# A mixture-of-experts layer on one core: block outputs added in memory, and the shared expert moved behind the routes

## The chip, the cores and the metric

The kernel runs on one core of one Trainium2 chip. The metric is the device time of the whole kernel in microseconds (us). It is a chain of eight layers (four pairs of a mixing layer and a feed-forward layer); the change touches the last layer only.

## The reference, cut to what matters

The input of the last layer, `x`, is 4096 tokens of 256 numbers. Each token goes to the two of eight experts that score highest, and all tokens go to a shared expert; the sum is normalised and added to `x`.

```
xf = layernorm(x)                                   # 4096 x 256
scores = softmax(xf @ w_router)                     # 8 experts
expert_weights, expert_indices = top_k(scores, 2)
cw[token, expert_indices] += expert_weights
h  = silu(xf @ w1[e]) * (xf @ w3[e])                # hidden 512, each expert e
moe_out = sum_e cw[:, e] * (h @ w2[e])
shared  = silu(xf @ ws1) * (xf @ ws3) @ ws2
out = shared / 3 + moe_out * 2 / 3
x = x + layernorm(out)
```

All numbers are 32-bit floats.

## The kernel before, in words

The 4096 tokens are held as eight batches `b` of 512, each a tile of 128 partitions by 4 rows by 256 (`K.X[b]`). The code is written in program order; the order of the instructions on each engine's queue is set afterwards by a planner that takes what it expects to be ready first. Every engine works through its own queue in that order. The loads and stores are issued from SP's queue, the indirect ones (gather and scatter by a list of row numbers) from POOL's.

`l3_ffn` has four stages.

1. Routes. `route(b)` (L1772) normalises the batch on DVE (L1777), transposes it on PE (`norm_T`, L146, copied out by ACT at L148), multiplies by the router (L1783), and takes softmax and the two best experts on ACT and DVE (L1788 to L1804). In the one-hot tiles `O[0]` and `O[1]` it marks which expert is the first and which the second choice of each token; the two weights times 2/3 stay in `G2[b]`. For the first five batches (`EARLY = 5`) `shared(b, ...)` follows: `experts` with the shared weights (matmuls `gs` at L1740, silu on ACT at L1745, product on DVE at L1746), `down` (matmuls `ys` at L1754), and a copy times 1/3 by ACT into `acc[b]`, a tile that stays on the chip (L1877).
2. Sort. `places()` works out on PE and DVE for every token and choice a row in a list sorted by expert, in which each expert fills whole blocks of 256 rows (`rows`, written at L1857), and the expert of each of the 39 blocks (`ei`, L1870). Then 64 scatters on POOL's queue (L1939) write the normalised rows to `xs` in memory, 128 rows of 1 KB each. Before that `xs`, 39 x 256 rows, is cleared by one store from ACT's queue (L1717). SP loads the 39 expert numbers into registers meanwhile (L1887).
3. Blocks. `block(j, ei)` for 39 blocks: the weights of the block's expert (three loads of 512 KB, L1725) and its 256 rows (`xb`, L1893, which waits for all 64 scatters) are loaded; PE transposes the rows (L1900), `experts` and `down` follow, ACT copies the result out of PSUM (L1907), and POOL's queue stores it to `ys` in memory (L1908).
4. The last three batches' shared expert, with weights loaded anew, the rows transposed anew, and the result laid over the batch's normalised rows (`xnr`); then `combine(b)` for all eight batches: eight gathers from `ys` (L1916), each multiplied by its weight and added by DVE (L1919), and `K.add_norm` (L164 to L174: statistics on DVE, scaling on ACT at L172, addition to `X[b]` on POOL at L174). The batch is stored at L1975.

The PSUM pool of `gs` and `gb` has four buffers, that of `ys` and `yb` two; the tiles `xb` and `yb` have two buffers, the hidden tile of the shared expert one.

An earlier layer, `l1_ffn`, already adds its results to rows in memory: L1250 scatters 128 rows of 1 KB with `compute_op=ALU.add` to `out_d`, once for each of 48 experts, and each of these waits for the one before. Its `late(b)` loads the rows back at L1257.

`K.stats` (L99 to L119) has two ways to the inverse root: three Newton steps on DVE, or, where `K.log_exp` is set, Ln and Exp on ACT (L111, L112) and three small DVE instructions (L113 to L115).

Of the kernel before, what the change touches and what calls it, by code (L numbers as in the profile page):

```python
# [9 lines left out]
F32 = mybir.dt.float32  # L10
# [10 lines left out]
NB = 8  # L21
# [1671 lines left out]
def l3_ffn(K):  # L1693


    nc, tc = K.nc, K.tc
    w = K.W["l3_ffn"]
    wr = w[:, 0:16].rearrange("p (k n) -> p k n", k=2)
# [5 lines left out]
    with ExitStack() as es:  # L1704
        def pool(name, bufs, **kw):
            return es.enter_context(tc.tile_pool(name="f3" + name, bufs=bufs, **kw))
        dr = pool("dr", 1, space=DRAM)
        xs = dr.tile([NBLK * BK, D], F32, name="xs")
        ys = dr.tile([NBLK * BK, D], F32, name="ys")
        cst, wp, sb, s1, s3 = pool("c", 1), pool("w", 2), pool("a", 2), pool("b", 1), pool("d", 3)  # L1710
        pmm = pool("pm", 2, space=PSUM)
        pG = pool("pg", 4, space=PSUM)
        pY = pool("py", 2, space=PSUM)

        zero = cst.tile([P, D], F32, name="zero")
        nc.vector.memset(zero, 0.0)
        cleared = nc.scalar.dma_start(  # L1717
            out=xs.rearrange("(n p) d -> p n d", p=P),
            in_=zero[:, None, :].to_broadcast([P, NBLK * BK // P, D]))

        def load_weights(src, uid, sel):
            ts = []
# [37 lines left out]
            return load_weights([i["l3f_s1"], i["l3f_s3"], i["l3f_s2"]], uid, lambda s: s)  # L1760


        XN, O, G2, acc = [], [], [], []
        for j in range(2):
            O.append(cst.tile([P, E, TT], F32, name=f"O{j}"))
        xTs = {}

        def feature_major(b):
            return K.norm_T(b, s1, pmm, "mm", xn=XN[b])

        def route(b):
            xn = cst.tile([P, NT, D], F32, name=f"xnr{b}")  # L1772
            XN.append(xn)
            x = K.X[b]
            mv, r = K.stats([x[:, n, :] for n in range(NT)], "ln")
            for n in range(NT):
                nc.vector.tensor_scalar(  # L1777
                    xn[:, n, :], x[:, n, :], mv[:, n, 0:1], r[:, n:n + 1], ALU.subtract, ALU.mult)
            t = feature_major(b)
            pl = pmm.tile([P, NT, E], F32, tag="mm", name=f"pl{b}")  # L1780
            for n in range(NT):
                for k in range(2):
                    nc.tensor.matmul(  # L1783
                        pl[:, n, :], lhsT=t[:, k, n * P:(n + 1) * P], rhs=wr[:, k, :],
                        start=(k == 0), stop=(k == 1))
            g = sb.tile([P, NT, E], F32, tag="g", name=f"g{b}")
            m = sb.tile([P, NT], F32, tag="m", name=f"m{b}")
            nc.vector.tensor_reduce(m, pl, AX.X, ALU.max)  # L1788
            nc.vector.tensor_tensor(g, pl, m[:, :, None].to_broadcast([P, NT, E]), ALU.subtract)
            nc.scalar.activation(g, g, AF.Exp)  # L1790
            nc.vector.tensor_reduce(m, g, AX.X, ALU.add)
            nc.vector.reciprocal(m, m)
            nc.vector.tensor_tensor(g, g, m[:, :, None].to_broadcast([P, NT, E]), ALU.mult)
            v8 = cst.tile([P, NT, 8], F32, name=f"v8{b}")
            i8 = sb.tile([P, NT, 8], U32, tag="i8", name=f"i8{b}")
            for n in range(NT):
                nc.vector.max(v8[:, n, :], g[:, n, :])
                nc.vector.max_index(i8[:, n, :], v8[:, n, :], g[:, n, :])
            f8 = sb.tile([P, NT, 8], F32, tag="f8", name=f"f8{b}")
            nc.vector.tensor_copy(f8, i8)  # L1800
            nc.vector.tensor_scalar(v8, v8, 2.0 / 3.0, None, ALU.mult)
            G2.append(v8)
            for j in range(2):
                nc.vector.tensor_tensor(  # L1804
                    O[j][:, :, b * NT:(b + 1) * NT].rearrange("p e n -> p n e"),
                    iota[:, None, :].to_broadcast([P, NT, E]),
                    f8[:, :, j:j + 1].to_broadcast([P, NT, E]), ALU.is_equal)
            return t

        def places():  # L1810
# [40 lines left out]
            for j in range(2):  # L1851
# [4 lines left out]
                r = cst.tile([P, TT], U32, name=f"row{j}")  # L1856
                nc.vector.tensor_copy(r, f)  # L1857
                rows.append(r)
            jt = cst.tile([1, NBLK], I32, name="jt")
            nc.gpsimd.iota(jt, [[1, NBLK]], base=0, channel_multiplier=0)  # L1860
            jf = cst.tile([1, NBLK], F32, name="jf")
            nc.vector.tensor_copy(jf, jt)
            ge = cst.tile([1, NBLK, E - 1], F32, name="ge")
            nc.vector.tensor_tensor(
                ge, jf[:, :, None].to_broadcast([1, NBLK, E - 1]),
                end[0:1, None, 0:E - 1].to_broadcast([1, NBLK, E - 1]), ALU.is_ge)
            ef = cst.tile([1, NBLK], F32, name="ef")
            nc.vector.tensor_reduce(ef, ge, AX.X, ALU.add)
            ei = cst.tile([1, NBLK], I32, name="ei")
            nc.vector.tensor_copy(ei, ef)  # L1870
            return rows, ei

        def shared(b, t, ws, a):
            hT = experts(t, L, ws, f"s{b}")
            for half in range(2):
                ps = down(hT, (2 * half, 2 * half + 1), ws[2], f"s{b}_{half}")
                nc.scalar.activation(  # L1877
                    a[:, 2 * half:2 * half + 2, :], ps, AF.Copy, scale=1.0 / 3.0)

        def after(ins, earlier):  # L1880
            tc.add_manual_dep(
# [1 line left out]
                mybir.DependencyInfo(mybir.DependencyClass.Sync, mybir.DependencyReason.DATA),  # L1883
                reason="rows written by it")

        def block(j, ei):
            e = nc.values_load(  # L1887
                ei[0:1, j:j + 1], engines=[mybir.EngineType.SP], min_val=0, max_val=E - 1)
            ws = load_weights(
                [i["l3f_w1"], i["l3f_w3"], i["l3f_w2"]], f"b{j}",  # L1890
                lambda s: s[bass.ds(e, 1)].rearrange("o d n -> (o d) n"))
            xb = sb.tile([P, 2, D], F32, tag="xb", name=f"xb{j}")
            ld = nc.sync.dma_start(  # L1893
                out=xb, in_=xs[j * BK:(j + 1) * BK].rearrange("(n p) d -> p n d", p=P))
            for sc in sorted_:
                after(ld, sc)
            ps = pmm.tile([P, 2, BK], F32, tag="mm", name=f"pxb{j}")
            for k in range(2):
                for n in range(2):
                    nc.tensor.transpose(  # L1900
                        ps[:, k, n * P:(n + 1) * P], xb[:, n, k * P:(k + 1) * P], K.ident)
            xT = sb.tile([P, 2, BK], F32, tag="xbT", name=f"xbT{j}")
            nc.vector.tensor_copy(xT, ps)
            hT = experts(xT, BK, ws, f"b{j}")
            ps = down(hT, (0, 1), ws[2], f"b{j}")
            y = sb.tile([P, 2, D], F32, tag="yb", name=f"yb{j}")
            nc.scalar.copy(y, ps)  # L1907
            nc.gpsimd.dma_start(  # L1908
                out=ys[j * BK:(j + 1) * BK].rearrange("(n p) d -> p n d", p=P), in_=y)

        def combine(b, a, rows):
            for n in range(NT):
                for j in range(2):
                    y = s3.tile([P, D], F32, tag=f"yg{j}", name=f"yg{b}_{n}_{j}")
                    col = b * NT + n
                    nc.gpsimd.indirect_dma_start(  # L1916
                        out=y, out_offset=None, in_=ys[:, :],
                        in_offset=bass.IndirectOffsetOnAxis(ap=rows[j][:, col:col + 1], axis=0))
                    nc.vector.scalar_tensor_tensor(  # L1919
                        a[:, n, :], y, G2[b][:, n, j:j + 1], a[:, n, :], ALU.mult, ALU.add)  # L1920
            K.add_norm(b, [a[:, n, :] for n in range(NT)], s1)

        EARLY = 5
        ws = shared_weights("sh0")
        for b in range(NB):
            t = route(b)
            if b < EARLY:
                acc.append(cst.tile([P, NT, D], F32, name=f"acc{b}"))  # L1930
                shared(b, t, ws, acc[b])
        rows, ei = places()

        sorted_ = []
        for b in range(NB):
            for n in range(NT):
                col = b * NT + n
                for j in range(2):
                    sc = nc.gpsimd.indirect_dma_start(  # L1939
                        out=xs[:, :],  # L1940
                        out_offset=bass.IndirectOffsetOnAxis(ap=rows[j][:, col:col + 1], axis=0),
                        in_=XN[b][:, n, :], in_offset=None)
                    after(sc, cleared)
                    if sorted_:
                        tc.declare_no_dep(sc.ins, group="f3xs", reason="distinct rows")
                    tc.add_to_no_dep_group("f3xs", sc.ins)
                    sorted_.append(sc)
        for j in range(NBLK):
            block(j, ei)
        ws = shared_weights("sh1")  # L1950
        for b in range(EARLY, NB):
            acc.append(XN[b])
            shared(b, feature_major(b), ws, acc[b])
        for b in range(NB):
            combine(b, acc[b], rows)


LAYERS = (("l0_attn", load_l0_attn, l0_attn), ("l0_ffn", load_l0_ffn, l0_ffn),
# [97 lines left out]
```

## Time and profile before

| what | value |
|---|---|
| time, median of 3 runs | 5448.51 us (5447.48 to 5449.12) |
| the profiled execution's own time | 5451.61 us |
| its span, first to last instruction | 5449.9 us |
| granted TensorE clock, mean over the span | 0.915 |
| PE busy over the span | 4489.4 us, 82% |
| DVE / ACT / POOL busy | 3018.0 / 1886.3 / 1875.6 us |
| last layer: first instruction | about 4624 us |
| 64 scatters of the sort (L1939) | 4785.6 to 4866.4 us |
| first block's first matmul record (L1900) | 4873.9 us |
| last block's last matmul record (L1754) | 5319.5 us |
| end of the span | 5449.9 us |

The last layer is 825.9 us of the span, from 4624.0 to the end. A line such as "L1939 POOL DMA_INDIRECT xs<-xnr,row" gives the line of the code, the engine, the operation and the tiles written and read; a stretch in square brackets is the idle time ahead of the instruction and what ended it. A 32-bit matmul of the program shows as two PE records. The time for which POOL is busy with a DMA is that of issuing it; the data lands later.

### The profile page before, as it was taken

The page shows a single profiled execution, that of the slowest core. Times are in us where ns is not written, and L with a number is a line of the kernel's source. Part 1 is how long each engine was busy: PE and PEld are TensorE (multiplying, and loading weights), DVE is VectorE, ACT ScalarE, POOL GpSimd, SP SyncE. Part 2 cuts the span into 40 slices and gives each one's busy share as a digit, 9 for nine tenths or more (in the row PEclk, how much of TensorE's full clock was granted, in tenths as well). Part 3 has the DMA queues.
Part 4 walks back from the last instruction along what each step waited for, and adds up shares of the span by engine and source line. Part 5 has one row for each costly group of instructions (what it writes and reads, how often), then busy time and mean ns, then how long its engine had stood idle before and what let it go on. Part 6 is the DMA issues. An engine that isn't in the chain of part 4 may idle for free.

```text
span 5449.9 us, 55804 instructions
## 1 busy us (share of the span) xinstructions
PE 4489.4 (82%) x18546; PEld 2726.0 (50%) x18546; DVE 3018.0 (55%) x8220; ACT 1886.3 (35%) x3752; POOL 1875.6 (34%) x1218
## 2 busy tenths in 40 slices
PE   8655888999975978888888899788888887929996
PEld 3334765655554964444444455333333333528883
DVE  6999555467684125554555533377777777211115
ACT  5401324343331323333333224455555553201112
POOL 0001213443433341111111000388888887040005
PEclk9777889999997988999999999899999998969997
DMA  4386501000014960000000000011111111136653
GB/s 117 87 202 147 145 26 41 5 9 5 9 38 131 249 179 8 5 5 4 5 5 1 1 19 0 25 48 47 45 45 44 44 44 64 58 124 185 186 180 95
DMA packets 405477, 364.67 MB, mean 67 GB/s; under 512 B 209762, under 2 KB 338996, under 8 KB 404628
## 3 DMA queue, kind: packets, MB, share of 16 engines
q1 hardware_dynamic: 364740, 294.03, 19.6%
q0 software_dynamic: 18768, 40.04, 2.6%
q10 hardware_dynamic: 21680, 27.02, 1.5%
q8 instruction: 147, 2.41, 0.2%
q14 instruction: 142, 1.16, 0.1%
HBM read 279.35 MB, written 81.43 MB: 66 GB/s over the span
## 4 chain that ended last, share of the span: by engine, by line
PE 30%; DVE 15%; issue 12%; POOL 6%; ACT 5%; DMA 1%; POOLq 0%; DVEq 0%; another core or an unknown queue 0%; ACTq 0%; SPq 0%
DVE h L1667 6%; PE T L1402 4%; PE S L1379 3%; PE h L1234 3%; PE g L1495 3%; PE y L1638 3%; DVE junk L1384 2%; DVE dB L1613 2%; PE py L185 2%; POOL h L1670 2%; PE pc L1560 2%; PE y L1245 2%; PE o L1411 1%; ACT PT L1405 1%; PE gs L1740 1%
## 5 line engine op out<-in xcount | busy, mean ns | idle before, releaser
L1670 POOL TENSOR_TENSOR h<-h,C 128x1024 f32<-128x1024 f32 x256 | 595.7, 2354 | 176.0 <-DVE h L1667 140.1
L1638 PE MATMUL y<-h,C 128*128 128x512 f32 x1024 | 533.3, 662 | 106.4 <-POOL h L1670 106.4
L1667 DVE TENSOR_TENSOR_SCAN h<-dA,dB 128x512 f32<-128x512 f32 x512 | 589.0, 1203 | 29.3 <-ACT dA L1664 11.5
L1664 ACT ACTIVATE dA<-dl,A 128x512 f32<-128x512 f32 x512 | 352.6, 691 | 411.0 <-DVE h L1667 400.9
L1638 PEld LDWEIGHTS y<-h,C 128*128 128x128 f32 x1024 | 202.1, 208 | 414.6 <-issue 224.2
L929 POOL TENSOR_SCALAR p<-p,rs 128x128 f32<-128x128 f32 (+3 forms) x256 | 275.7, 1086 | 384.6 <-DVE rs L928 222.1
L1379 PE MATMUL S<-KT,qz 128*128 128x512 f32 (+3 forms) x1024 | 350.1, 479 | 40.9 <-ACT qz L1367 21.3
L174 POOL TENSOR_TENSOR X<-X,yn 128x1024 f32<-128x1024 f32 x64 | 150.7, 2355 | 587.9 <-ACT yn L172 526.8
L1405 ACT ACTIVATE PT<-T 128x256 f32<-128x256 f32 (+3 forms) x512 | 211.4, 437 | 387.0 <-PE T L1402 379.1
L1402 PE MATMUL T<-qz,KT 128*128 128x512 f32 (+3 forms) x1024 | 310.5, 446 | 2.9 <-DVE mx L1384 0.3
L1407 POOL TENSOR_SCALAR_AFFINE_SELECT PT<-PT 128x512 f32<-128x512 f32 x128 | 81.2, 635 | 631.5 <-ACT PT L1405 628.0
L1618 POOL TENSOR_TENSOR dB<-du,B 128x2048 f32<-128x2048 f32 x64 | 289.6, 4526 | 0.1
L1379 PEld LDWEIGHTS S<-KT,qz 128*128 128x128 f32 x1024 | 184.6, 198 | 209.3 <-DVE mx L1384 55.9
L1384 DVE CUSTOM_DVE_ANT_0 junk<-S,mask 128x256 f32<-128x256 f32 (+3 forms) x512 | 250.3, 489 | 61.5 <-PE S L1379 16.2
L1740 PE MATMUL gb<-xbT,w_b 128*128 128x256 f32 x1248 | 277.8, 381 | 7.5 <-issue 7.5
L1740 PEld LDWEIGHTS gb<-xbT,w_b 128*128 128x128 f32 x1248 | 235.9, 190 | 43.1 <-ACT yb L1907 11.4
L1613 DVE TENSOR_TENSOR dB<-du,pb 128x2048 f32<-128x2048 f32 x64 | 145.4, 2273 | 167.7 <-PE pb L1610 118.1
L1402 PEld LDWEIGHTS T<-qz,KT 128*128 128x128 f32 x1024 | 169.9, 191 | 132.8 <-issue 85.1
L1746 DVE TENSOR_TENSOR hTb<-sb,gb 128x512 f32<-128x512 f32 x78 | 53.6, 687 | 298.2 <-PE gb L1740 298.2
L927 ACT ACTIVATE p<-p,nm 128x128 f32<-128x128 f32 (+3 forms) x256 | 143.8, 563 | 197.0 <-DVE nm L923 192.3
L1239 ACT ACTIVATE hT<-h,w_l_ffn 128x128 f32<-128x128 f32 x384 | 109.5, 367 | 221.0 <-PE h L1234 221.0
L1234 PE MATMUL h<-xgT,w 128*128 128x128 f32 x1536 | 185.2, 279 | 0.0
(472 smaller groups left out, 9073.7 us busy)
## 6 DMA issues: line engine op xcount, KB each, us to landing
w_b<-l3f_w SPq DMA_DIRECT2D x117, 512.0 KB
w<-l1f_w SPq DMA_DIRECT2D x48, 1024.0 KB
C<-xdd SPq DMA_DIRECT2D x128, 256.0 KB
B<-xdd SPq DMA_DIRECT2D x64, 256.0 KB
w<-l1f_w SPq DMA_DIRECT2D x48, 256.0 KB
toep<-l0fd SPq DMA_DIRECT2D x32, 320.0 KB
xs<-zero ACTq DMA_DIRECT2D x1, 9984.0 KB
xb<-xs SPq DMA_DIRECT2D x39, 256.0 KB
```

The lines of the kernel that those rows point to most:

```text
L929: nc.gpsimd.tensor_scalar(p[:, 0:n], p[:, 0:n], rs, None, ALU.mult)
L1234: nc.tensor.matmul(ph[:, j, :], lhsT=w1[:, s, c, m * P:(m + 1) * P], rhs=xgT[:, c, :], start=(c == 0), stop=(c == 1))
L1379: nc.tensor.matmul(ps[:, 0:n], lhsT=QZ[:, j, qt * P:n], rhs=KT[:, g, 0:n], start=True, stop=True)
L1384: nc.vector.tensor_tensor_reduce(out=junk[:, 0:n], in0=tiles[j][:, 0:n], in1=mask[:, L - n:L], scale=1.0, scalar=-3.0e38, op0=ALU.add, op1 ...
L1402: nc.tensor.matmul(ps[:, 0:n], lhsT=KT[:, g, kt * P:(kt + 1) * P], rhs=QZ[:, j, kt * P:L], start=True, stop=True)
L1405: nc.scalar.activation(PT[:, j, :], ps[:, 0:n], AF.Exp)
L1618: nc.gpsimd.tensor_tensor(dB, du, B[:, None, :].to_broadcast([P, 4, L]), ALU.mult)
L1638: nc.tensor.matmul(py[2 * j + c], lhsT=K.ident, rhs=h[:, c, :], start=False, stop=(n == NS - 1))
L1664: nc.scalar.activation(dA, dl[:, c, :], AF.Exp, scale=A[:, c, n:n + 1])
L1667: nc.vector.tensor_tensor_scan(hs[-1][:, c % 2, :], dA, dB[:, c, :], 0.0, ALU.mult, ALU.add)
L1670: nc.gpsimd.tensor_tensor(h, h, C[:, None, :].to_broadcast([P, 2, L]), ALU.mult)
L1740: nc.tensor.matmul(ps[:, q, :], lhsT=ww[:, k, (c + q) * P:(c + q + 1) * P], rhs=xT[:, k, :], start=(k == 0), stop=(k == 1))
```

## The change

The last layer is put together in another way.

- The rows that are scattered carry four more numbers each: the token's number, the difference of its two weights, the second weight, and the number of its first expert (`R_ID`, `R_DW`, `R_W1`, `R_E0`). So the rows of `xs`, of `xb` and of the normalised batch are 260 numbers long, 1040 bytes. The cleared rows carry the numbers of padding rows behind the last token.
- There is no `ys` and no `combine`. `acc` is now a list in memory with a row for each token. `shared(b)` stores a third of the shared expert's result there. `block(j)` works out each row's weight (the first choice's if the block's expert is the row's first expert, otherwise the second's), ACT multiplies by it while it copies out of PSUM, in two halves, and two scatters with `compute_op=ALU.add` add the halves to the tokens' rows of `acc`.
- All eight routes come first, then `places()`, the scatters, all eight shared experts, the blocks. The transposed batches of 0 to 4 stay in a pool of five, those of 5 to 7 in a free part of the weights' memory; nothing is transposed twice and the shared weights are loaded once.
- At the end the eight batches of `acc` are loaded and go through `add_norm` with `K.log_exp` set.
- The tiles `xb`, `yb` and the new `wt` and `it` have three buffers.

The diff, cut to its core:

```diff
-        xs = dr.tile([NBLK * BK, D], F32, name="xs")
-        ys = dr.tile([NBLK * BK, D], F32, name="ys")
+        R_ID, R_DW, R_W1, R_E0, R_END = D, D + 1, D + 2, D + 3, D + 4
+        xs = dr.tile([NBLK * BK, R_END], F32, name="xs")
+        acc = dr.tile([NB * L + P, D], F32, name="acc")
+        sx = pool("x", 5)
...
+        nc.sync.dma_start(out=acc[NB * L:NB * L + P, :], in_=zero[:, 0:D])
+        zi = cst.tile([P, 1], I32, name="zi")
+        nc.gpsimd.iota(zi, [[1, 1]], base=NB * L, channel_multiplier=1)
+        nc.vector.tensor_copy(zero[:, R_ID:R_ID + 1], zi)
...
-            t = feature_major(b)
+            dst = spare[:, b - 5] if b >= 5 else None
+            t = K.norm_T(b, sx, pmm, "mm", xn=xn, dst=dst)
...
-            G2.append(v8)
+            nc.gpsimd.tensor_copy(xn[:, :, R_ID], ti[:, b * NT:(b + 1) * NT])
+            nc.vector.tensor_tensor(xn[:, :, R_DW], v8[:, :, 0], v8[:, :, 1], ALU.subtract)
+            nc.gpsimd.tensor_copy(xn[:, :, R_W1], v8[:, :, 1])
+            nc.gpsimd.tensor_copy(xn[:, :, R_E0], f8[:, :, 0])
...
-        def shared(b, t, ws, a):
+        def shared(b, t, ws):
             hT = experts(t, L, ws, f"s{b}")
+            a = sb.tile([P, NT, D], F32, tag="acc", name=f"acc{b}")
             for half in range(2):
                 ps = down(hT, (2 * half, 2 * half + 1), ws[2], f"s{b}_{half}")
                 nc.scalar.activation(
                     a[:, 2 * half:2 * half + 2, :], ps, AF.Copy, scale=1.0 / 3.0)
+            nc.sync.dma_start(
+                out=acc[b * L:(b + 1) * L].rearrange("(n p) d -> p n d", p=P), in_=a)
...
+            xb = s3.tile([P, 2, R_END], F32, tag="xb", name=f"xb{j}")
             ld = nc.sync.dma_start(
                 out=xb, in_=xs[j * BK:(j + 1) * BK].rearrange("(n p) d -> p n d", p=P))
             for sc in sorted_:
                 after(ld, sc)
+            wt = s3.tile([P, 2], F32, tag="wt", name=f"wt{j}")
+            nc.vector.scalar_tensor_tensor(
+                wt, xb[:, :, R_E0], ef[:, j:j + 1], xb[:, :, R_DW], ALU.is_equal, ALU.mult)
+            nc.vector.tensor_tensor(wt, wt, xb[:, :, R_W1], ALU.add)
+            it = s3.tile([P, 2], U32, tag="it", name=f"it{j}")
+            nc.vector.tensor_copy(it, xb[:, :, R_ID])
...
-            nc.scalar.copy(y, ps)
-            nc.gpsimd.dma_start(
-                out=ys[j * BK:(j + 1) * BK].rearrange("(n p) d -> p n d", p=P), in_=y)
+            y = s3.tile([P, 2, D], F32, tag="yb", name=f"yb{j}")
+            for n in range(2):
+                nc.scalar.activation(y[:, n, :], ps[:, n, :], AF.Copy, scale=wt[:, n:n + 1])
+                nc.gpsimd.indirect_dma_start(
+                    out=acc[:, :], out_offset=bass.IndirectOffsetOnAxis(ap=it[:, n:n + 1], axis=0),
+                    in_=y[:, n, :], in_offset=None, compute_op=ALU.add)
...
-        EARLY = 5
-        ws = shared_weights("sh0")
-        for b in range(NB):
-            t = route(b)
-            if b < EARLY:
-                acc.append(cst.tile([P, NT, D], F32, name=f"acc{b}"))
-                shared(b, t, ws, acc[b])
-        rows, ei = places()
+        ws = shared_weights("sh")
+        spare = K.wslot("spare_attn")[:, 0:3072].rearrange("p (b k n) -> p b k n", b=3, k=2)
+        ts = [route(b) for b in range(NB)]
+        rows, ef, ei = places()
...
+        for b in range(NB):
+            shared(b, ts[b], ws)
         for j in range(NBLK):
-            block(j, ei)
-        ws = shared_weights("sh1")
-        for b in range(EARLY, NB):
-            acc.append(XN[b])
-            shared(b, feature_major(b), ws, acc[b])
+            block(j)
+        K.log_exp_tables()
+        K.log_exp = True
         for b in range(NB):
-            combine(b, acc[b], rows)
+            y = sx.tile([P, NT, D], F32, tag="xT", name=f"yl{b}")
+            nc.sync.dma_start(
+                out=y, in_=acc[b * L:(b + 1) * L].rearrange("(n p) d -> p n d", p=P))
+            K.add_norm(b, [y[:, n, :] for n in range(NT)], sb)
+        K.log_exp = False
```

More of the change, by code (lines that the diff above doesn't have):

```diff
@@ L1713, in l3_ffn @@
         pY = pool("py", 2, space=PSUM)
-        zero = cst.tile([P, D], F32, name="zero")
+        zero = cst.tile([P, R_END], F32, name="zero")
         nc.vector.memset(zero, 0.0)
+        nc.sync.dma_start(out=acc[NB * L:NB * L + P, :], in_=zero[:, 0:D])
+        zi = cst.tile([P, 1], I32, name="zi")
+        nc.gpsimd.iota(zi, [[1, 1]], base=NB * L, channel_multiplier=1)
+        nc.vector.tensor_copy(zero[:, R_ID:R_ID + 1], zi)
         cleared = nc.scalar.dma_start(
             out=xs.rearrange("(n p) d -> p n d", p=P),
-            in_=zero[:, None, :].to_broadcast([P, NBLK * BK // P, D]))
+            in_=zero[:, None, :].to_broadcast([P, NBLK * BK // P, R_END]))
+        ti = cst.tile([P, TT], I32, name="ti")
+        nc.gpsimd.iota(ti, [[P, TT]], base=0, channel_multiplier=1)
         def load_weights(src, uid, sel):
@@ L1760, in shared_weights @@
             return load_weights([i["l3f_s1"], i["l3f_s3"], i["l3f_s2"]], uid, lambda s: s)
-        XN, O, G2, acc = [], [], [], []
+        XN, O = [], []
         for j in range(2):
             O.append(cst.tile([P, E, TT], F32, name=f"O{j}"))
-        xTs = {}
-        def feature_major(b):
-            return K.norm_T(b, s1, pmm, "mm", xn=XN[b])
         def route(b):
-            xn = cst.tile([P, NT, D], F32, name=f"xnr{b}")
+            xn = cst.tile([P, NT, R_END], F32, name=f"xnr{b}")
             XN.append(xn)
@@ L1777, in route @@
                 nc.vector.tensor_scalar(
-                    xn[:, n, :], x[:, n, :], mv[:, n, 0:1], r[:, n:n + 1], ALU.subtract, ALU.mult)
-            t = feature_major(b)
+                    xn[:, n, 0:D], x[:, n, :], mv[:, n, 0:1], r[:, n:n + 1], ALU.subtract, ALU.mult)
+            dst = spare[:, b - 5] if b >= 5 else None
+            t = K.norm_T(b, sx, pmm, "mm", xn=xn, dst=dst)
             pl = pmm.tile([P, NT, E], F32, tag="mm", name=f"pl{b}")
@@ L1793, in route @@
             nc.vector.tensor_tensor(g, g, m[:, :, None].to_broadcast([P, NT, E]), ALU.mult)
-            v8 = cst.tile([P, NT, 8], F32, name=f"v8{b}")
+            v8 = sb.tile([P, NT, 8], F32, tag="v8", name=f"v8{b}")
             i8 = sb.tile([P, NT, 8], U32, tag="i8", name=f"i8{b}")
@@ L1858, in places @@
                 rows.append(r)
-            jt = cst.tile([1, NBLK], I32, name="jt")
+            jt = cst.tile([P, NBLK], I32, name="jt")
             nc.gpsimd.iota(jt, [[1, NBLK]], base=0, channel_multiplier=0)
-            jf = cst.tile([1, NBLK], F32, name="jf")
-            nc.vector.tensor_copy(jf, jt)
-            ge = cst.tile([1, NBLK, E - 1], F32, name="ge")
+            jf = cst.tile([P, NBLK], F32, name="jf")
+            nc.gpsimd.tensor_copy(jf, jt)
+            ge = cst.tile([P, NBLK, E - 1], F32, name="ge")
             nc.vector.tensor_tensor(
-                ge, jf[:, :, None].to_broadcast([1, NBLK, E - 1]),
-                end[0:1, None, 0:E - 1].to_broadcast([1, NBLK, E - 1]), ALU.is_ge)
-            ef = cst.tile([1, NBLK], F32, name="ef")
+                ge, jf[:, :, None].to_broadcast([P, NBLK, E - 1]),
+                end[:, None, 0:E - 1].to_broadcast([P, NBLK, E - 1]), ALU.is_ge)
+            ef = cst.tile([P, NBLK], F32, name="ef")
             nc.vector.tensor_reduce(ef, ge, AX.X, ALU.add)
             ei = cst.tile([1, NBLK], I32, name="ei")
-            nc.vector.tensor_copy(ei, ef)
-            return rows, ei
-        def shared(b, t, ws, a):
+            nc.vector.tensor_copy(ei, ef[0:1, :])
+            return rows, ef, ei
+        def shared(b, t, ws):
             hT = experts(t, L, ws, f"s{b}")
+            a = sb.tile([P, NT, D], F32, tag="acc", name=f"acc{b}")
             for half in range(2):
@@ L1884, in after, with block @@
                 reason="rows written by it")
-        def block(j, ei):
+        def block(j):
             e = nc.values_load(
@@ L1891, in block @@
                 lambda s: s[bass.ds(e, 1)].rearrange("o d n -> (o d) n"))
-            xb = sb.tile([P, 2, D], F32, tag="xb", name=f"xb{j}")
+            xb = s3.tile([P, 2, R_END], F32, tag="xb", name=f"xb{j}")
             ld = nc.sync.dma_start(
@@ L1905, in block @@
             ps = down(hT, (0, 1), ws[2], f"b{j}")
-            y = sb.tile([P, 2, D], F32, tag="yb", name=f"yb{j}")
-            nc.scalar.copy(y, ps)
-            nc.gpsimd.dma_start(
-                out=ys[j * BK:(j + 1) * BK].rearrange("(n p) d -> p n d", p=P), in_=y)
[L1911 to L1921, printed above, removed]
-        EARLY = 5
-        ws = shared_weights("sh0")
-        for b in range(NB):
-            t = route(b)
-            if b < EARLY:
-                acc.append(cst.tile([P, NT, D], F32, name=f"acc{b}"))
-                shared(b, t, ws, acc[b])
-        rows, ei = places()
+            y = s3.tile([P, 2, D], F32, tag="yb", name=f"yb{j}")
[8 more added lines that the diff above has]
+        rows, ef, ei = places()
         sorted_ = []
```

## The prediction, put on record before the changed kernel ran

> **What bounds the kernel now.** I read the stage windows of the last layer first, then the timeline of its seams, then the one place earlier in the kernel where the added operation already runs. The columns of the first view are PE, weight loads, DVE, ACT and POOL busy time, the granted clock, DMA share and GB/s.
>
> ```profile
> 4624.00:4785.60 161.60, 140.56 (x516) 91.05 (x516) 58.54 (x339) 41.88 (x65) 0.11 (x1) 0.88 0.19 64
> 4785.60:4873.90 88.30, 0.01 (x1) 0.04 (x1) 0.00 (x0) 0.00 (x0) 61.55 (x64) 0.50 0.39 137
> 4873.90:5319.50 445.60, 437.77 (x2034) 370.90 (x2035) 78.86 (x117) 69.41 (x117) 27.22 (x38) 1.00 0.59 179
> 5319.50:5449.90 130.40, 82.16 (x213) 45.33 (x210) 70.48 (x252) 29.27 (x56) 81.39 (x73) 0.78 0.33 99
> ```
>
> Four stages, each with its own limit: routes with five shared experts (PE), the sort (POOL alone, PE idle), 39 expert blocks (PE, 98%), and three shared experts with the combine, where no engine is full. Together 825.9 us.
>
> ```profile
> 4785.62 1.06 POOL L1939 DMA_INDIRECT xs<-xnr,row  x1 [161.50 <-DVE row L1857]
> ...
> 4865.41 0.96 POOL L1939 DMA_INDIRECT xs<-xnr,row  x1 [0.30 <-issue]
> 4872.37 3.85 SPq L1893 DMA_DIRECT2D xb<-xs  x4
> 4873.89 1.94 PE L1900 MATMUL pxb<-C,xb 128*128 128x128 f32 x8 [93.97 <-DMA xb<-xs]
> ```
>
> The sort is 64 scatters at 1.265 us; PE waits 94 us for its end. SP's 39 register loads (L1887) run beside it, 4785.6 to 4865.4.
>
> ```profile
> 1801.24 1.57 POOL L1250 DMA_INDIRECT out_d<-yw,iT  x1 [0.76 <-DVE yw L1249]
> 1805.81 0.99 POOL L1220 DMA_INDIRECT xg<-xn_d,iT  x1 [2.99 <-PE pxg L1225]
> 1808.17 1.56 POOL L1250 DMA_INDIRECT out_d<-yw,iT  x1 [1.37 <-DMA out_d<-yw,iT]
> ```
>
> L1250 is an accumulating scatter of 128 rows x 1 KB, exactly what the change adds. The third line was held by the first one's data: 6.93 us from start to start, at a DMA share above 0.9.
>
> ```profile
> 5362.11 2.36 POOL L174 TENSOR_TENSOR X<-X,yn 128x1024 f32<-128x1024 f32 x1
> 5362.59 2.18 DVE L1919 SCALAR_TENSOR_TENSOR acc<-yg,v,acc 128x256 f32<-128x256 f32 x1 [1.68 <-DMA yg<-ys,row]
> ...
> 5441.48 2.34 POOL L174 TENSOR_TENSOR X<-X,yn 128x1024 f32<-128x1024 f32 x1 [8.03 <-ACT yn L172]
> 5443.85 0.37 SPq L1975 DMA_DIRECT2D out<-X  x1
> ```
>
> A DVE instruction that usually takes 0.48 us takes 2.18 beside POOL's add; and 6.1 us pass from the last store's issue to the span's end.
>
> **What the Trainium skill says.** "PSUM — Partial Sum Buffer", section Engine vs sequencer instructions: the queues of ScalarE, VectorE and GpSimd are strictly first in, first out. The trace agrees (POOL's 1808.17 line held everything after it). "DMA: Bandwidth & Descriptors", section Rules for kernel authors: an accumulating DMA reads its target and writes it later, so the next one on the same bytes must wait for its semaphore; the 1808.17 line shows that wait. Same page, section Anatomy of one DMA: about 2 us fixed cost, mostly the write receipt; L1250's case (1.56 us of POOL, then 3 to 5 us) is dearer. "SBUF — State Buffer", section Who interferes with whom: a DVE instruction with two SBUF inputs contends with a GpSimd instruction that reads SBUF; the 2.18 us agree.
>
> **The change, part by part** (stage sums against this execution's span of 5449.9; its own time is 5451.6, so 1.7 lie around the span; the median of the runs, 5448.5, is 3.1 below its own time).
>
> *Routes.* Four shared experts leave this stage. One costs PE 32 gs matmul records of 0.43 (13.7 us) and 32 ys records of 0.215 (6.9): 20.6; the period of a route with its shared expert is 23.9 (4656.3, 4680.1, 4704.0), a route being some 3.2. So 4 x 20.7 = 82.8 off, 78.8 left. What is late next: in the built order shared expert 0 stays woven into the routes, so ACT alternates between silu and exp for four rounds (table load 1.28 each way, L1745 and L1790) and each route waits on ACT, PE, DVE in turn. 0 to 12 us for that; I take 4. Stage: 83. The clearing of xs took 31 us (4625.3 to 4656.3, trace's DMA packets); even doubled by 1040-byte rows it ends near 4687, before the first scatter at about 4707. The small POOL copies (24 of 128x4) and the two iotas hide under the routes; uncovered, some 0.2 us each, 5 us.
>
> *Sort.* The same 64 scatters and 39 register loads: 88.3. Rows are 1040 bytes instead of 1024. The trace has no such scatter; bounds are 0.96 us (same descriptors) and 1.56 (L1250's price): 0 to +38 us. A gain is excluded, as the number of rows is the same. I take 0. SP's queue now also holds the stores of acc0 and acc1 among the loads; both are ready before, so nothing waits.
>
> *Shared experts under the sort.* The words of the change promise that 147 us of PE work fill the hole. The built order says otherwise: on DVE, the three small weight instructions of blocks 0 to 2 (after's L1914 to L1918), which wait for xb, stand ahead of shared expert 3:
>
> ```
> L1757 TensorTensor hTs2<-ss2_3,gs2_3_1 128x512
> L1914 TensorScalarPtr wt0<-xb0,ef 128x2      [waits for the load of xb0]
> ...
> L1757 TensorTensor hTs3<-ss3_0,gs3_0_1 128x512
> ```
>
> xb0 waits for all scatters. So DVE stands from about expert 2's end until the sort is over; ACT (silu of 3) and PE (out of PSUM buffers: four, two of which only DVE frees) stop behind it. Under the sort lie experts 1, 2 and five eighths of 3's gs. After it remain 5.1 + 6.9 + 4 x 20.7 = 94.8, and 1.2 to restart: 96 us exposed. Nobody else is hurt: POOL is in its scatters, and acc2's store, queued behind xb0 on SP, has two buffers of slack.
>
> *Blocks.* PE work unchanged: 445.6. Per block ACT gets two scaled copies instead of one (some 0.2 us more), DVE three tiny ones (3 x 0.16): both under 20% busy, hidden; uncovered, 39 x 0.7 = 27 us. POOL loses a 0.72 us write and gets two accumulating scatters, each waiting for the one before. Two of them must fit into 445.6 / 39 = 11.4 us, so 5.71 each. From L1250: the 48 starts are 6.3 us apart, mostly unhindered, so usually under 6.3; by the packets the data lands 4.35 us after the start on average (3.35 to 6.2), and the two held ones restarted 1.1 us after landing: 5.4 at a DMA share above 0.9. Here the share is 0.59, some 0.7 with the adds. Bounds 4.4 (quickest landing) and 6.93: 0 to +95 us; a gain is excluded, since PE is full. I take 5.0, hidden. The first weights of block 1 wait for expert 7's last use of theirs; they have 19 us (expert 7's ys, block 0) for a load of about 8.
>
> *Tail.* Gone: three shared experts, 64 gathers, 64 DVE adds: 130.4. New: ACT 0.8; two last adds 2 x 5 = 10; load of yl0 3.8 (an equal load, L1257, took that to its reader); norm with ACT's Ln/Exp: bn 1.7 + 0.5, ACT 0.5, DVE 0.7, ACT 2.1, gaps 0.2: 5.7; POOL's eight adds 2.36 and then seven at a spacing between 2.36 (POOL full) and 5.5 (DVE and ACT shut out during each add); I take 3.3, since the built order lets DVE run two batches ahead: 23.1; store 6.1. Sum 52 (45 to 67).
>
> Sum: 83 + 88.3 + 96 + 445.6 + 52 = 764.9 against 825.9: 61 off. Span 5388.9, own time 5390.6, and at the median's place 3.1 lower: 5387.5 us.
>
> **The rivals.**
> *The adds become the bound (slower side).* Place: POOL's queue in the block stage, 78 serial adds. Point: above 5.71 us each it costs, at (445.6 + 61) / 78 = 6.5 the gain is gone. At the seen 6.93 for all: 78 x 6.93 = 540.5, +95: 5482. For: weight loads come in bursts, and writes of ys in this stage landed up to 6.3 after issue. Against: the mean of 5.4 was reached at a higher DMA share, and three yb buffers even out single late ones. A milder form, 6.0 each, gives +22: 5410.
> *Wider rows cost POOL 1.56 each:* 64 x 0.6 = 38 more sort, only idle PE beneath: 5426.
> *The weight instructions don't hold DVE* (the change does what it says): 147.5 of shared work from the first scatter, 88.3 covered, 59 left instead of 96: 5350. Against: the built order.
>
> **How the numbers follow.** Forecast 0.66 (own range 5367 to 5408: routes -4/+8, tail -7/+15, combined), wide rows 0.12, adds mildly late 0.08, adds beyond 6.5 us 0.07, full cover 0.07. The range 5350 to 5428 leaves out the slow rival, half of the full cover and the tails. About 0.2% (11 us) is what a measurement of this kernel can tell from no change: faster 0.91, same 0.02 (adds near 6.5), slower 0.07.
>
> **What would show it.** Routes: first xs scatter near 4707. Sort: still 1.27 us per scatter. DVE: an idle of some 45 us before wt0, released by xb0's load; shared experts 3 to 7 after it, first block near 4891. Blocks: 22.7 us per pair, POOL idle between adds released by ACT yb; if by the adds themselves, the first rival holds. Tail: some 52 us from PE's last matmul. The prediction is wrong if the scatter price or the adds' spacing leaves its bounds, or if DVE isn't held.

## The result and the profile after

The changed kernel takes 5615.92 us (median of 4 runs, 5615.01 to 5630.74), the kernel before 5448.82 (4 runs): a ratio of 1.0312, 95% interval 1.0295 to 1.033. It is 167 us slower, where 61 us less had been forecast. The profiled execution is the longest of the four, 5630.74 us with a span of 5628.9, which is 179.0 more than the span of before; the table below adds up to these 179, not to 167.

First the stage windows of the changed kernel, cut at the forecast's seams: routes, sort (up to DVE's first weight instruction), shared experts still to do, blocks (first transpose to PE's last matmul), tail. Columns as before: PE, weight loads, DVE, ACT, POOL, granted clock, DMA share, GB/s.

```profile
4629.60:4702.50 72.90, 57.87 (x277) 41.53 (x278) 48.32 (x333) 26.56 (x41) 4.54 (x28) 0.80 0.49 152
4702.50:4787.50 85.00, 42.78 (x132) 24.71 (x130) 4.71 (x7) 7.76 (x13) 61.51 (x64) 0.78 0.38 131
4787.50:4887.50 100.00, 96.61 (x300) 57.87 (x301) 14.82 (x29) 15.52 (x26) 0.00 (x0) 0.96 0.13 40
4887.50:5579.20 691.70, 515.50 (x2029) 425.19 (x2027) 94.52 (x225) 79.01 (x155) 118.33 (x76) 0.85 0.45 114
5579.20:5628.90 49.70, 0.02 (x1) 0.00 (x0) 21.47 (x96) 21.02 (x51) 21.68 (x10) 0.54 0.56 174
```

| term | before | forecast | after | after less before |
|---|---|---|---|---|
| start of the layer | 4624.0 | same | 4629.6 | +5.6 |
| routes | 161.6 | 83 | 72.9 | -88.7 |
| sort | 88.3 | 88.3 | 85.0 | -3.3 |
| shared experts left over | | 96 | 100.0 | +100.0 |
| blocks | 445.6 | 445.6 | 691.7 | +246.1 |
| tail | 130.4 | 52 | 49.7 | -80.7 |
| sum | | | | +179.0 |

Four terms came within some 10 us, and they alone would have made the kernel faster. The whole surprise is in one row: the same 2030-odd matmul records that filled 445.6 us at a clock of 1.00 now take 691.7, with PE busy for 515.5 of them and a mean granted clock of 0.85. The block stage is no longer PE's.

The timeline of the changed kernel over one block, from the middle of the stage, shows the cycle (weight loads left out):

```profile
5212.40 1.55 POOL L1931 DMA_INDIRECT acc<-yb,it  x1 [10.98 <-ACT yb L1930]
...
5218.32 1.56 POOL L1931 DMA_INDIRECT acc<-yb,it  x1 [4.36 <-DMA acc<-yb,it]
...
5219.87 1.03 PE L1765 MATMUL yb<-w_b,hTb 128*128 128x256 f32 x4
5224.28 0.17 DVE L1918 CAST it<-xb 128x2 uint32<-128x2 f32 x1 [6.91 <-DMA acc<-yb,it]
5224.38 0.69 DVE L1757 TENSOR_TENSOR hTb<-sb,gb 128x512 f32<-128x512 f32 x1
5225.12 4.41 PE L1765 MATMUL yb<-w_b,hTb 128*128 128x256 f32 x12 [4.23 <-DVE hTb L1757]
5229.37 7.07 PE L1751 MATMUL gb<-xbT,w_b 128*128 128x256 f32 x32
5229.57 0.84 ACT L1930 ACTIVATE yb<-yb,wt 128x256 f32<-128x256 f32 x2 [10.64 <-PE yb L1765]
5230.32 1.55 POOL L1931 DMA_INDIRECT acc<-yb,it  x1 [10.44 <-ACT yb L1930]
```

Read it from POOL's first line to its last. The block's first add starts at 5212.40; the second waits until the first one's data has landed and starts 5.92 us later; 5.96 us after that a tiny DVE instruction, the copy of row numbers into `it`, starts, and what it waited for was the second add. Directly behind it on DVE stands the second half of the product `hTb`; PE waited 4.23 us for that; then the rest of `yb`, ACT's copy, and the next block's first add at 5230.32. The cycle is closed: 5.92 + 5.96 + 0.84 (to PE's restart) + 4.45 (yb to ACT) + 0.75 = 17.92 us, and over the stage the period is 17.88, against the 11.4 that PE's work takes (445.6 / 39).

The built order of DVE's queue says why (order, tile, waits):

```
L1757 hTb4 (first half)                 [waits PE, ACT]
L1918 it6<-xb6                          [waits both adds of block 3]
L1757 hTb4 (second half)                [waits PE, ACT]
```

`it` has three buffers. The scheduler makes it as soon as `xb` is there, two blocks ahead; so `it6` takes over the buffer of `it3`, and must wait until the adds of block 3 have read it, only one block back. The three buffers are used up by running ahead, and the wait stands in front of work that is due now.

The groups of `yb` matmuls, of the kernel before (L1754) and of the changed one (L1765), and the acc tile's list of those who waited for it (us, times), with the adds' time to landing, give the sum:

```profile
L1754 PE MATMUL yb<-w_b,hTb 128*128 128x256 f32 x624 | 150.9, 386 | 0.3 <-DVE hTb L1746 0.3
L1765 PE MATMUL yb<-w_b,hTb 128*128 128x256 f32 x624 | 228.4, 532 | 167.9 <-DVE hTb L1757 167.9
```

```profile
  DVE it L1918: 263.8, 36
  POOL acc L1931: 105.5, 27
...
DMA to landing us min/median/max: 3.6/5.4/6.8
```

So 167.9 - 0.3 = 167.6 us are holes and 228.4 - 150.9 = 77.5 are the same matmuls taking longer: 245.1 of the 246.1. The second part is the clock. The windows of the changed kernel around one hole:

```profile
5199.00:5202.00 3.00, 2.95 (x14) 2.26 (x12) 0.00 (x0) 0.60 (x1) 1.56 (x1) 1.00 0.39 128
5202.00:5206.30 4.30, 0.00 (x0) 0.00 (x0) 0.77 (x2) 0.00 (x0) 0.00 (x0) 0.78 0.73 185
5206.40:5208.00 1.60, 1.60 (x4) 1.33 (x5) 0.00 (x0) 0.00 (x0) 0.00 (x0) 0.50 0.00 0
...
5210.00:5212.00 2.00, 2.00 (x10) 1.66 (x9) 0.00 (x0) 0.34 (x1) 0.00 (x0) 0.69 0.00 0
5212.90:5215.00 2.10, 2.10 (x10) 1.87 (x11) 0.77 (x3) 0.11 (x1) 1.06 (x1) 1.00 0.74 252
```

A hole of 4.3 us (second line), then half clock for between 4 and 5 us, then full again. The Trainium skill, "TensorE: Matmul & The Clock Gate", Part 1, says that PE falls to half its clock after an idle window of about 3.4 us and comes back after about as long of work. These lines agree roughly; but 3.4 us is no safe limit for a hole, since in the run with plain writes (below) holes of 2.3 us were followed by half clock too.

At the sort's seam the trace has what the forecast read from the built order. DVE stood 57 us for xb0, and PE 45.6 us behind it; the scatters cost what they did:

```profile
4782.26 0.96 POOL L1946 DMA_INDIRECT xs<-xnr,row  x1 [0.30 <-issue]
...
4787.52 0.22 DVE L1914 SCALAR_TENSOR_TENSOR wt<-xb,ef 128x2 f32<-128x2 f32 x1 [56.94 <-DMA xb<-xs]
...
4790.89 7.35 PE L1751 MATMUL gs<-xT,w_sh 128*128 128x512 f32 x12 [45.61 <-DVE hTs L1757]
```

### The profile page after: what moved, and what is told of

Read it like the earlier page. It is cut to its first block, busy times and chain, and to the rows that moved or that the text cites. A ratio compares the mean times of both kernels' runs of the same rounds, so it can differ in the third digit from the quotient of the medians.

```text
span 5628.9 us, 55853 instructions
## 1 busy us (share of the span) xinstructions
PE 4546.7 (81%) x18522; PEld 2767.8 (49%) x18522; DVE 2994.8 (53%) x8201; ACT 1895.7 (34%) x3800; POOL 1911.0 (34%) x1220
## 5 line engine op out<-in xcount | busy, mean ns | idle before, releaser
L1765 PE MATMUL yb<-w_b,hTb 128*128 128x256 f32 x624 | 228.4, 532 | 167.9 <-DVE hTb L1757 167.9
L1931 POOL DMA_INDIRECT acc<-yb,it x78 | 121.4, 1557 | 681.3 <-ACT yb L1930 405.2
L1765 PEld LDWEIGHTS yb<-w_b,hTb 128*128 128x128 f32 x624 | 167.5, 275 | 218.1 <-DVE hTb L1757 183.5
L1613 DVE TENSOR_TENSOR dB<-du,pb 128x2048 f32<-128x2048 f32 x64 | 145.5, 2274 | 171.3 <-PE pb L1610 121.6
```

Source lines behind the costliest of these rows:

```text
L1765: nc.tensor.matmul(ps[:, j, :], lhsT=hT[:, c, n * P:(n + 1) * P], rhs=w2[:, c, :], start=(c == 0), stop=(c == 3))
```

## The experiments

Theory: the wait of `it` for the adds of one block ago, in DVE's queue ahead of hTb, closes the loop; PE's half clock after each hole is its second half. Rivals: the adds' own chain on POOL is the bound; the clock is a throttle of its own; the new order does the harm. Each ratio below is to the kernel before on the same chip in the same batch (before: 5443.72, 5446.21, 5460.55, 5461.47 and 5444.84 us in the five batches).

| run | time, us | ratio to before (95%) |
|---|---|---|
| it: eight buffers | 5378.28 | 0.9883 (0.9862 to 0.9905) |
| it on POOL | 5378.23 | 0.9881 (0.9864 to 0.9897) |
| plain writes for adds | 5508.67 | 1.0117 (1.01 to 1.0134) |
| it and wt on POOL | 5340.80 | 0.9815 (0.9799 to 0.9832) |
| the same, adds doubled | 5666.98 | one run |
| first part alone, gathers | 5410.31 | 0.9935 (0.9918 to 0.9952) |
| it: four buffers | 5614.01 | 1.0318 (1.03 to 1.0335) |
| ten matmuls in the hole | 5696.67 | 1.0463 (1.0446 to 1.0481) |
| five matmuls in the hole | 5588.96 | 1.0231 (1.0207 to 1.0256) |
| it, wt on POOL; stores on ACT | 5400.82 | 0.9899 (0.9883 to 0.9914) |
| it, wt on POOL; three acc buffers | 5334.10 | 0.979 (0.9776 to 0.9803) |
| it, wt on POOL, again | 5353.34 | 0.9827 (0.9813 to 0.9841) |

**More buffers for `it`.**

```diff
-            it = s3.tile([P, 2], U32, tag="it", name=f"it{j}")
+            it = si.tile([P, 2], U32, tag="it", name=f"it{j}")   # si = pool("i", 8)
```

> Changed: the row numbers `it` get a pool of eight buffers of their own; nothing else. Theory (the wait of DVE's `it` for the adds of one block ago stands ahead of hTb and closes a loop of 18 us per block): the 4.3 us holes of PE ahead of yb, released by DVE hTb, go; PE is full again in the block stage, or nearly (the adds' own chain, 78 x 5.0 to 5.9 us, is 390 to 460); block stage 446 to 470 instead of 695, time 5366 to 5395 us. In the built order `it` of the block four ahead now stands ahead of some hTb and waits for its xb load instead; if that is late, a few us per pair of blocks come back (up to 5430). Rival 1 (the adds' chain in POOL's queue is the bound): no change of period, 5600 or more, POOL's adds released by the adds throughout. Rival 2 (the granted clock of 0.86 in the block stage is a throttle of its own): holes go but matmuls stay slow, block stage about 520, time 5440.

Measured: 5378.28 us. The window of the block stage and the yb group of this kernel (one line further down in the code):

```profile
4875.60:5320.20 444.60, 435.94 (x2029) 369.43 (x2027) 95.17 (x225) 79.00 (x155) 118.33 (x76) 1.00 0.70 178
```

```profile
L1766 PE MATMUL yb<-w_b,hTb 128*128 128x256 f32 x624 | 151.0, 386 | 0.3 <-DVE hTb L1758 0.3
```

444.6 us at clock 1.00, with 76 of the 78 adds issued in it: POOL still has 118.33 us of issuing, PE no holes. Rivals 1 and 2 of this run fall. The edit takes the ratio from 1.0312 to 0.9883, and the forecast's 5387.5 would have been close for this kernel. The feared wait for xb loads did not appear.

**The copy on POOL, three buffers as before.**

```diff
-            nc.vector.tensor_copy(it, xb[:, :, R_ID])
+            nc.gpsimd.tensor_copy(it, xb[:, :, R_ID])
```

> Changed: the copy of the row numbers is made by POOL instead of DVE, still with three buffers. Theory (what counts is DVE's queue, not the buffer): `it` of two blocks ahead stands in POOL's queue between adds that wait for the same landing anyway, DVE is free; block stage 446 to 470, time 5366 to 5395 us. Rival 1 (the adds' chain is the bound): 5600 or more, as after. Rival 3 (the reuse of three buffers is the bound wherever the copy stands): the period stays 18 us, 5600.

Measured: 5378.23 us, the block stage 444.2 (first transpose 4878.54, PE's end 5322.75). The buffer count is the same as in the slow kernel; only the queue differs. On POOL the copy stands between adds that wait for the same landing anyway. So the number of buffers need not change: it is enough that the wait stands in another queue than hTb.

**Four buffers.**

```diff
+        si = pool("i", 4)        # and it from si, as with eight
```

> Changed: the row numbers get four buffers instead of three. Theory with the built order: the scheduler uses the fourth buffer to copy one block further ahead, so that the copy which stands ahead of the second half of hTb still waits for the adds of the block just before; no gain, period 18 us, 5590 to 5620 us. Rival (each buffer more gives the adds one more block of slack): the wait is for adds of two blocks ago, 23 us, and is over in time; 5370 to 5400 us.

Measured: 5614.01 us, period 17.38. The yb group of this kernel:

```profile
L1766 PE MATMUL yb<-w_b,hTb 128*128 128x256 f32 x624 | 223.9, 523 | 153.4 <-DVE hTb L1758 153.4
```

The fourth buffer bought nothing: in this kernel's built order `it4` stands between the halves of hTb1 and waits for the adds of block 0. So the scheduler spends each buffer on running one block further ahead, until something else (xb) stops it. With eight, `it8` stands in hTb4 and waits for block 0.

**Plain writes.** The sums over a token's two blocks and its shared expert are left out.

```diff
-                    in_=y[:, n, :], in_offset=None, compute_op=ALU.add)
+                    in_=y[:, n, :], in_offset=None)
```

> Changed: the scatters of the block outputs write instead of adding (the sums are left out); order, waits and buffers as in the changed kernel. Theory of the loop: the loop stays and only its two DMA links get shorter, from 5.9 us each to between 3.5 and 5.3 (issue 0.96 instead of 1.56 us, no read of the target): 13.5 to 17 us per block, time 5430 to 5570 us. Rival (the adding itself, its reading of the target, is what costs): the period falls to PE's 11.4 us, time about 5370 us.

Measured: 5508.67 us, period 15.13 (POOL 0.96 us for each issue). The loop stays: PE still waits 96.6 us for hTb. Adding instead of writing costs 17.88 - 15.13 = 2.75 us per block in this loop, some 1.8 of them as longer holes ((167.9 - 96.6) / 39) and 0.9 as more time of matmuls at half clock (the yb group is 195.1 us here, 228.4 with adds); the loop itself is there with either.

This run also shows that shorter holes can halve the clock. Two holes of the same length, in square brackets, and the 12 records after them:

```profile
5090.19 4.54 PE L1765 MATMUL yb<-w_b,hTb 128*128 128x256 f32 x12 [2.30 <-DVE hTb L1757]
...
5163.61 2.86 PE L1765 MATMUL yb<-w_b,hTb 128*128 128x256 f32 x12 [2.34 <-DVE hTb L1757]
```

Of the 33 holes over 1.5 us in this stage 25 were followed by slow records and eight were not, and the length alone does not tell them apart: the shortest slow one is 1.95 us, the longest harmless one 3.55.

**The adds doubled.** On top of `it` and `wt` on POOL (below), each add is issued twice, so each block output counts twice.

> Changed against the version with `wt` and `it` on POOL: each accumulating scatter is issued twice (so each block output is added twice). It measures what the adds cost when they alone are the bound. Theory (adds are serial, one lands before the next starts, 5.0 to 5.9 us each): 156 x 5.0 to 5.9 = 780 to 920 us of block stage instead of 446, time 5675 to 5815 us. Rival (adds overlap, and the 5.9 us seen in the changed kernel is a latency and no price): 156 x 1.6 us of POOL's own work = 250, hidden; time 5340 as without the doubling.

Measured: 5666.98 us. The two groups of adds of this kernel, with first and last start:

```profile
L1932 POOL DMA_INDIRECT acc<-yb,it x78: 1550/1569/1656, 4873.1 to 5613.1; - x78
L1935 POOL DMA_INDIRECT acc<-yb,it x78: 1554/1573/1607, 4877.4 to 5617.0; - x78
```

155 intervals in 5617.0 - 4873.1 = 743.9 us: 4.80 us each, when nothing but adds is the bound (the time is 8 us below the expected range, one run). They are serial, and two of them, 9.6, fit into PE's 11.4. Here the stage is stretched, so the DMA engines have less to do beside the adds (share 0.53); in the kernel with eight buffers, at a share of 0.70, the second add of a block started 4.86 us after the first on average. The disputed price was right.

**The first part alone.** Routes first and shared experts under the sort, but ys and gathers as before (the adds, `it` and `wt` gone; xb and yb with two buffers again).

> The change's first part alone: all routes first and the shared experts under the sorting, as in the changed kernel, their sums kept in memory; but the block outputs are written to ys in sorted order and gathered by token at the end, as in the kernel before (no `wt`, no `it`, no adds). Theory (the adds of the changed kernel cost 250 us through DVE's queue alone, and the first part is a gain): routes 73, sort 81, 60 exposed, blocks 446, tail 45 + 64 gathers instead of 16 loads, between 20 and 60 us more than the 45: 5360 to 5400 us, below before. Rival (the loss comes from the new order, for instance from the clock after the long sort or from the shared experts' stores): block stage near 695, 5600.

Measured: 5410.31 us, a gain, though 10 above the range. Block stage and tail of this kernel:

```profile
4853.20:5297.50 444.30, 435.96 (x2030) 368.98 (x2027) 78.85 (x117) 69.46 (x117) 27.22 (x38) 1.00 0.59 179
5297.50:5419.60 122.10, 0.00 (x0) 0.00 (x0) 62.35 (x160) 22.48 (x50) 80.68 (x73) 0.52 0.40 118
```

The new order does no harm to the blocks. The tail is 122.1 us where the expectation allowed 65 to 105; with adds in memory it is 49.7. So the adds in memory are worth having once their wait stands elsewhere: 0.9935 of before here against 0.9815 with `it` and `wt` on POOL, below. (Without `wt` DVE isn't held under the sort in this kernel either: 145.5 us from the first scatter to the first block.)

**Matmuls in the hole.** Ten matmuls of 128x512, overwritten at once, ahead of each yb; then five.

```diff
+            for _ in range(fill):
+                nc.tensor.matmul(ps, lhsT=hT[:, 0, 0:P], rhs=w2[:, 0:2, :], start=True, stop=True)
```

> Changed: ten 128x512 matmuls whose result is overwritten stand ahead of the yb matmuls of each block, so PE works (some 4.3 us) where it stood idle; everything else as in the changed kernel, the loop too. Theory of the clock (the 0.50 granted right after each 4.3 us hole is an effect of the hole, and costs about 2.0 us per block in the yb matmuls): the clock stays near 1.0, yb's 12 matmuls take 2.8 us instead of 4.4 to 5.3, period 16 to 16.8 us: 5525 to 5560 us, faster with 390 more matmuls. Rival (the clock follows the work done or the power, not the hole): the same or slower, 5610 to 5650.

Measured: 5696.67 us, slower. I had taken a PE record of 0.43 us for a matmul; each such matmul is two records, as all others here. The filling took 8.75 us and ran 3 us past hTb, period 19.70. The clock did stay at 1.00. With half as many:

> Changed: five 128x512 matmuls, whose result is overwritten, ahead of the yb matmuls of each block instead of ten (each takes 0.88 us, twice what was reckoned for the ten: they overfilled the hole by 3 to 4 us). Theory of the clock (the hole causes the 0.50, which costs some 2 us per block): 4.4 us of filling fit the 4.3 us hole, the 16 yb matmuls take 3.6 us after it as with ten, the loop shortens to 15.5 to 16.5 us per block: 5510 to 5555 us, below the changed kernel although PE has 195 matmuls more. Rival (the half clock after the hole has another cause, or nothing is won because the adds set the period): within 10 us of the changed kernel.

Measured: period 16.16 us against 17.88; the block stage takes 630.6 us, 61 less than in the changed kernel, with 195 matmuls more. From its timeline:

```profile
5230.40 4.45 PE L1764 MATMUL yb<-w_b,hTb 128*128 128x512 f32 x10
...
5235.29 0.17 DVE L1920 CAST it<-xb 128x2 uint32<-128x2 f32 x1 [7.38 <-DMA acc<-yb,it]
...
5236.46 2.86 PE L1767 MATMUL yb<-w_b,hTb 128*128 128x256 f32 x12 [0.75 <-DVE hTb L1757]
```

The last line is what took 4.41 us in the changed kernel. PE had more work and still the full clock, so the hole makes the half clock. The whole time, 5588.96, is above the range: this chip ran the kernel before 12 us slower too, and the stage from the first scatter to the first block took 205 us instead of 185 (see the stores on ACT).

**Weights and row numbers on POOL.**

```diff
-            nc.vector.scalar_tensor_tensor(
-                wt, xb[:, :, R_E0], ef[:, j:j + 1], xb[:, :, R_DW], ALU.is_equal, ALU.mult)
-            nc.vector.tensor_tensor(wt, wt, xb[:, :, R_W1], ALU.add)
+            nc.gpsimd.tensor_scalar(
+                wt, xb[:, :, R_E0], ef[:, j:j + 1], None, ALU.is_equal)
+            nc.gpsimd.tensor_tensor(wt, wt, xb[:, :, R_DW], ALU.mult)
+            nc.gpsimd.tensor_tensor(wt, wt, xb[:, :, R_W1], ALU.add)
...
+            nc.gpsimd.tensor_copy(it, xb[:, :, R_ID])
```

> Changed: `it` and the three instructions of the weight `wt` (four of them, as the compare and the product are split) are made by POOL; DVE has nothing left that waits for xb ahead of the shared experts. Theory: the loop is gone as with `it` on POOL, and DVE no longer stands 57 us under the sort, so shared experts 3 to 7 run under it: of the 104 us between the last scatter and the first block some 45 go (PE's hole of 45.6 us), time 5320 to 5350 us. Rival (something else holds PE under the sort, its PSUM or acc buffers): the hole stays and the time is that of `it` on POOL alone. Rival (POOL's eight tiny instructions per pair lie between adds and lengthen the adds' chain): block stage 480 or more.

Measured: 5340.80 us, 37 less than with `it` alone on POOL. From first scatter to first block 148.0 us instead of 184.8. A smaller hole is left, in PE's timeline of this kernel:

```profile
4767.57 7.03 PE L1751 MATMUL gs<-w_spare_attn,w_sh 128*128 128x512 f32 x16
4782.81 9.46 PE L1751 MATMUL gs<-w_spare_attn,w_sh 128*128 128x512 f32 x16 [8.22 <-ACT ss L1756]
```

ACT waited 21.45 us there to write acc4, whose buffer the store of acc2 still held; and that store stands on SP behind the load of xb0. Two edits aim at it.

**Its stores on ACT's queue.**

```diff
-            nc.sync.dma_start(
+            nc.scalar.dma_start(
                 out=acc[b * L:(b + 1) * L].rearrange("(n p) d -> p n d", p=P), in_=a)
```

> Changed against the version with `wt` and `it` on POOL: the stores of the shared experts' sums to memory go through ACT's queue instead of SP's. In that version's trace they stand on SP behind the load of xb0, which waits for the whole sort; ACT's copy into acc4 waited 21 us for the store of acc2, and PE idled 8.2 us and then took 9.5 us for 16 gs matmul records instead of 6.9. Theory: that hole and the slow restart go, some 10 to 11 us; first block near 148 us after the first scatter's start minus 11 = 137 (of PE work: 137 to 139), time 5325 to 5335 us, ratio to before 0.978 to 0.980. Rival (the issue on ACT, eight of some 0.4 us, delays silu and what waits for it, or acc's two buffers still bind): no change, 0.981 to 0.983.

Measured: 5400.82 us, 0.9899 of before where 0.9815 was had without the edit. ACT's waits during the sort:

```profile
ACT acc L1890 <- issue: 36.5, 1, 36.5
ACT ss L1756 <- remote: 21.8, 1, 21.8
...
ACT ss L1756 <- issue: 10.6, 1, 10.6
```

None has a releaser that the profile shows, and PE stood for 42.1 us and DVE for 65.7 beside them. The run with five matmuls has the same three pauses on ACT (36.6, 21.8, 10.6), though its ACT queue is that of the changed kernel, and the changed kernel's own trace has none of them. Both ran on chips on which the kernel before took 5460 us instead of 5445. So this run doesn't price the edit, and the pauses stay unexplained.

**Three buffers for the shared experts' sums.**

```diff
-            a = sb.tile([P, NT, D], F32, tag="acc", name=f"acc{b}")
+            a = s3.tile([P, NT, D], F32, tag="acc", name=f"acc{b}")
```

(and xb, yb from `sb`, two buffers each, to make room)

> Changed against the version with `wt` and `it` on POOL: three buffers instead of two for the shared experts' sums (and two instead of three each for xb and yb, to make room). Theory (ACT waits 21 us there for the store of acc2, which stands behind xb0's load on SP, and PE idles 8.2 us): with a third buffer ACT's wait reaches the end of the sort one expert later, after xb0 is through; PE's hole and its slow restart go, first block 138 us after the first scatter instead of 148, 10 to 11 us faster than its neighbour in this batch. Rival (the wait for something else, or the smaller xb and yb buffers cost in the block stage what is won): the same time or slower than its neighbour.

> The version with `wt` and `it` on POOL once more, on the same chip as its neighbour in this batch, so that a difference of 10 us can be told: 0.9815 of before expected, 10 to 11 us above the version with three acc buffers; the rival expects no difference.

Measured: 5334.10 against 5353.34 us. The window from first scatter to first block, three buffers:

```profile
4713.10:4850.30 137.20, 137.20 (x432) 81.89 (x431) 18.48 (x28) 23.28 (x39) 63.02 (x72) 1.00 0.32 109
```

PE is busy for all of it: 137.2 instead of 148.4 us. That is 11.2 of the 19 us, and what was expected. Where the other 8 lie is not shown: block stage (444.2) and tail (50) are alike in the two traces, and the trace with three buffers is of the slowest of its five executions (5346.91 us), in which the sort even began 5.3 us later than in its neighbour's. This is the best version found, 2.1% faster than before.

## Why the prediction was wrong

*Blocks: the failed step.* "DVE three tiny ones (3 x 0.16): both under 20% busy, hidden" priced the added instructions by their work and asked how busy DVE is. What had to be priced was the third one's wait, and what is queued behind it: hTb, and PE behind that. A later sentence, on the adds as a rival, "three yb buffers even out single late ones", looked at the tile whose buffers the adds read most visibly; the adds read `it` as well, and `it` is written two blocks ahead, yb is not. The built order that the forecast quoted for the sort's seam has the same trap some 30 instructions further on. Measured: +246.1 us where 0 was put; with the wait moved to POOL, 444.2 (shown by the run with `it` on POOL).

*The adds.* Taken as 5.0 us and hidden; as the only bound they measure 4.80, and in the kernel with eight buffers they hid. The slow rival, "adds become the bound" above 5.71 us each, was wrong as to its mechanism: their throughput was never short. The sign that the forecast named for it did not come either: in the changed kernel POOL's idle time ahead of adds was ended mostly by ACT's `yb` (405.2 us, 38 times), less by the adds before (100.8 us, 26 times). It was their latency, 5.92 + 5.96 us, that came onto PE's path. No rival had that, so 0.07 was all that stood on the slow side.

*The clock.* The forecast had no term for it; 77.5 of the 246 us are PE at half clock after its holes (shown by the filling with five).

*Routes* were 10 us shorter than the 83 put down; the four rounds of silu and exp did not cost the 4 us taken for them, and why the rest went was not tried. *Sort*: 64 scatters at 0.96 us of issue, 79.7 us from the first start to the last (79.8 before); wider rows cost nothing, and that rival falls. *Shared experts left over*: 100.0 for 96, by the mechanism named; shown by moving `wt` to POOL, which gave 37 us. "Two buffers of slack" for acc2's store held in the changed kernel; it was the next thing in line once DVE was free. *Full cover* was put at 59 us after the sort and 5350 in all; with all waits moved PE runs without a gap and the time is 5334. *Tail*: 49.7 for 52.

## What to carry to other kernels

A small instruction is priced by what it waits for and by what stands behind it in its queue, not by its 0.17 us: for each buffer that a slow DMA reads, ask which earlier DMA its next writer waits for, how many blocks ahead that writer is placed, and what the same queue holds behind it. Here a fourth buffer was spent on running further ahead, and only eight helped; moving the writer to the queue that waits for that DMA anyway cost nothing (444.2 us of block stage). And holes in PE cost more than their own length: here 77.5 us of slow matmuls came on top of 167.6 us of holes.

## What the runs showed of the hardware that was not expected

- An accumulating scatter of 128 rows of 1 KB took POOL 1.56 us and landed 3.6 / 5.4 / 6.8 us (least, median, most) after its issue beside weight loads; as the only bound, with weight loads beside them still, they follow each other at 4.80 us. As plain writes in the same loop: 0.96 us and 2.4 / 4.4 / 6.6.
- Rows of 1040 bytes scatter at the price of 1024: 0.96 us each, 1.27 apart.
- PE at 0.50 after each of the 36 holes of the changed kernel (2.99 to 5.77 us): 12 yb records in 4.31 to 5.49 us instead of 2.86. With plain writes the same followed most holes of 2 to 3 us, but not all. Filling the hole with work that is thrown away shortened the loop.
- On two chips ACT paused for 36.5, 10.6 and 21.8 us under the scatters, with no releaser in the profile; the cause is open.
